# Cross-attention with an adapter branch: the adapter's weighted sums are turned by TensorE and divided in PSUM, instead of by VectorE's 32x32 blocks and a trip through HBM, in a new instruction order

## The chip, the cores and the metric

The kernel runs on one core of one Trainium2 chip. A core has five engines with a queue each: TensorE (PE in the profile, its weight loads PEld), VectorE (DVE), ScalarE (ACT), GpSimd (POOL) and SyncE (SP), which here issues nearly all DMAs. Every queue is worked off in its own order; an instruction that waits holds up everything behind it on its engine. The metric is the device time of one execution in microseconds (us), the median of several runs; the profile is a recording of one further execution.

## The reference, cut to what matters

Two sequences of 2048 rows of 640 numbers (`x`) attend to 124 text tokens each, and a second branch, the adapter, attends from 4 extra tokens to the whole of `x` and is used again. Everything is float32.

```python
query = hidden_states @ Wq
keyt, valt = enc @ Wk, enc @ Wv
hs = _mha(query, keyt, valt)                      # text branch, 8 heads
ca_q1 = jnp.einsum('btc,th->bch', ca, Wq_ca)      # 384 channels of 4 tokens
indices = np.linspace(0, CAD - 1, S).astype(np.int64)
ca_q1 = ca_q1[:, indices, :]                      # 2048 rows, only 384 different
ca_hs1 = _mha(ca_q1, residual, residual)          # first softmax of the adapter, over 2048 keys
ca_q2 = ca_hs1 @ Wq
ca_k2, ca_v2 = ca @ Wk_ca, ca @ Wv_ca
ca_hs2 = _mha(ca_q2, ca_k2, ca_v2)                # second softmax, over 4 tokens
out = (hs + ca_hs2) @ Wout + b_out + residual
```

## The kernel before, in words

**Two branches, 16 units.** Each of the two sequences (b = 0, 1) is cut into four blocks of 512 rows and eight text units of 256 rows (m = 0 to 15, `text`). A unit has scores (`sc`), a softmax (`p`, `r`), a turn of the probabilities by way of HBM (`eb`, `kept`, `pT`), a product with the values (`ph`, copied to `hs`), and the product with `Wout` (`po`), whose pieces VectorE adds to the residual rows (`x_more`, `last_rows`) before they are stored. The queries (`pq`) and the output product use sums of blocks of the operands, so that 7 products do the work of 8.

**The adapter** (`adapter`, L1474) goes through five stages for each b. (1) Scores of the 384 distinct channel rows against the 2048 keys, in 24 pieces of 128x2048 that fill a PSUM region of four banks (`s`); VectorE takes the maximum of each piece (`mx<-s`). (2) The maxima are turned by four 32x32 block transposes on VectorE (`spread`, L1510), sent to HBM and brought back as rows of the operand `cop`. (3) For each half j = 0, 1 of the heads, twelve pieces of scores (`s<-zop,cop`) get their exponential from ScalarE (`ea<-s`), and `contract` (L1584) multiplies them with `y_sb` into one PSUM bank `acc` of 128x384. Its 128 rows are four groups g of 32, in each of which 24 rows are weighted sums (`Y`) and one row is the sum of the exponentials (`ONE`); its columns are the 384 channels. (4) `second` (L1645) needs the channels on the partitions: it adds the sums over groups and halves, which gives the scores `s2f` of the second softmax (over 4 tokens). (5) The probabilities `p2t` are spread over the 2048 rows by a product with a 0/1 matrix (`pt_p<-rows,p2t`), copied, and stored to HBM (`p<-rows`), from where every unit's `pT` fetches its 4 extra rows (`second_rows`, L1867). So no `ph` product of sequence b can run before stage 5 of `adapter(b)`.

**Stages 3 to 4 in the kernel before.** At the end of each `contract(b, j)` VectorE turns `acc` in 32x32 blocks out of PSUM into `accs` (L1607), which frees the bank; then it takes the reciprocals of the exponentials' sums (L1613) and multiplies (L1614), into `prod[:, j]`. Since the blocks are turned each in its place, a channel's four groups still lie on four different partition quarters. So `second` adds the two halves (`both`, L1654), stores them to HBM (`heads_away`, L1662), fetches them back so that all four groups of a channel lie on one partition (`gather`, four DMAs, L1667; the buffer `heads` is the second half of `prod`), and sums them (`less`, L1674: three reductions, a maximum, a subtraction). ScalarE's exponential, a sum, a reciprocal and a product (`share`, L1687) follow, all before PE's `product` (L1706). This happens once for each b.

**The order** of all instructions is written out in the string `ORDER` (L74): 2240 numbers, each the number of a task (a Python generator) whose next step is to be issued; a letter a, v or g chooses the engine where two could do it. Tasks are numbered in the order in which they begin; 36 is `adapter(0)`, 241 is `adapter(1)` in both versions, and 37 + 4m is unit m's `text`, whose `probabilities` (loads of `pT`, then the `ph` products) is 40 + 4m. `Room` objects stand for buffers: there are four single PSUM banks (`banks`) beside the four-bank region until the second adapter is through (`more`, L1699), and two buffers `eas` for `ea` and `accs`.

**Matmul forms.** `Desk.matmul` (L205) issues a product with more than 64 rows and columns as four strips of 32 columns ("128*32" in the profile), except straight after a transpose or another product in the full 128*128 form; then it stays in that form until a product with a smaller shape.

Of the kernel before, what the change touches and what calls it, by code (L numbers as in the profile page):

```python
# [8 lines left out]
F32 = mybir.dt.float32  # L9
# [5 lines left out]
P = 128  # L15
# [51 lines left out]
class Desk:  # L67
# [7 lines left out]
        0 4 4 0 36 2 0 0 0 0 0 0 0 0 0 0 0 0 2 4 2 2 2 4 4 2 2 2 2 2 2 2 2 111v 6 6 6 0 0 112v 6 4 6 3 110 107 109 108  # L75
        4 114a 113a 3a 3 6 3a 3 115v 4 6 7 7 7 7 15 2 15 15 15 12 15 15 15 3v 1 3 116a 117a 8 7 8 11 15 15 10 7 7 7 7
        15 120a 5 6 118a 8 8 9 119v 14 7 7 7 7 121a 123v 8 7 7 36 122a 125a 8 124v 6 8 9 8 8 8 126 5 9 8 8 127 8 5 9 9
        9 36 5 129 14 15 128 130 9 9 9 14 14 14 14 9 6 6 135v 14 134a 133a 132v 14g 14 15 14 12 14g 15 136 36 36 6 11
        6 36 12 12 137 137 137 137 11a 36 15 137 36 36 15 12 12 36 145v 36 9 9 9 140 11 9 9 9 138a 139a 9 144a 12 13
        101 101g 101g 101g 101g 106 141 141 141 141 141 6 141 141 18 142 16 141 141 143 106 18 18 143 131 131 131 131  # L80
        143 143 143 39 146 146 36 36 146 146 146 146 17 17 101g 101v 101 147g 148g 150g 149g 146 143 131 151 17 155a
        17 146g 101g 36 18 18 18 18 18 143 36 101g 16 16 16 16 16 16 151 157a 156 16v 43 36 151 17 159a 156 156 158
        158 158 158 16 16 158 16g 36 146 151 160a 18 156 18 18 18 18 18 152 154 161 36 17 36 154 152 36 154 143 162
        162 162 162 162 18 20 19 21 21 21 21 146 158 156 20 163 36 162 158 164 19 36 36 153 171 36 19 143 19 19 19 19
        177a 167g 168g 170g 158g 178 43 171 153 36 158 36 179 179 181 36 180a 19g 171 165 166 21 21 166 166 21 21 21
        172 166 178 158 179 179 179 179 182a 178 39 183 19 183 21 21 179 179g 169g 36 21 21 21 21 20 23 178 166 183
        183 183 183 19 20 171 20 174 20 176 174 19g 17 166 166 166 22 36 36 179 183 184a 166 173 185 178 185 185 185
        185 24 24 24 179 185 186 183g 36 187 22 24 24 24 24 190 24 24 188 183 183 22 22 22 176 36 47 176 175 22 36 193
        193 193 36 175 194 193 22 193 193 24 173 173 173 173 23 200 23 23 36 204a 193 195 47 36 23 196g 197g 22g 200
        23 198g 193g 199g 24 24 22 24 24 205 205 24 207 20 173 26 173 173 173 205 205 205 22 22g 205 193 36 207 207  # L90
        207 207 203 210a 206a 189 156 207 205 192 36 51 203 36 36 189 27 27 193 27 27 27 27 205g 205 205 189 189 189
        27 192 203 200 213 213 213 213 36 189 215v 213 213 214 213 192 189 201 36 36 200 202 216 201 202 55 213g 213
        217 218 51 219 219 36 27 27 27 26 223g 221g 222g 27 220 220 36 219 219 219 219 219 192 192 189 189 220 220 220
        220 219g 224g 213 225 226 229a 36 227 225 227 226 191 131 156 131 191 131 191 208 191 191 231a 27 27 27 23 156
        36 219 36 27 220 30 232 36 219 220g 55 230a 228 225 36 191 234a 191 26 191 25 29 178 30 30 30 228 233 233 220
        220 156 30 235 225 228 36 36 36 233 191 36 36 209 233 233 233 36 131 36 211 209 59 237 236 238 233 238 233v
        233 25 238 238 25 25 36 238 238 26 59 26 36g 131 209 209 29 36 36 26 242v 243g 25 25 209 209 233 178 240 240
        240 240 36 209 209 209 247 246 238 245v 252v 36 247 36 240 247 246 36 247 253v 246 240 30 30 30 156 30 244v
        238g 212 192 238 238 212 254v 248 248 36 247 247 36 248 248 248 36 246 250 212 239 239 212 248 240 240g 212
        178 257a 36 63 36 212 247 250 247 247 247 36 30 30 239 240 239 260 260 260 260 260 212 30 30 261 25 260 36 30  # L100
        260 30 251 67 36 262 212 247 251 247 251 240 178 192 192 25 178 260g 260 260 10 192 36 36 263 263 264 212 263
        263 263 36 255 258 52 256 32 26 247 31 247 33 33 192 256 32 239 247 29 31 33 36 247 263 31 36 67 36 247 247 31
        36 29 36 29 247 247 29 270 31 271 263 265g 270 263v 263 270 270 36 270 270 36 256 256 256 256 247 272 272 272
        272 272 266v 272 63 277 277 271 33 267v 263 36 247 269 281v 277 277 277 256 36 36 247 247 269 33 31 33 33 11
        33 33 31 256 36 36 256 259 282 282 36 282 277 283v 271 269 36 36 282 249 271 282 282 259 31 247 271 259 259
        270 270v 270 270 259 275 31 31 28 247 247 284v 269 285v 36 249 28 36 36 282 282 31 28 36 286 268v 277 277v 31g
        241 28 71 28 287 28 259 282 36 282 259 36 280 36 288 277 288 289 282 25 25 277 288 288 36 288 25 288 282 280
        282 36 280 282 75 36 36 259 33 282 32 68 33 33 33 33 33 241 259 36 25g 290 288 288v 241 291 291 288 32 282 241
        282 282 32 241 36 32 31 288 273 31 291 291 291 291 36 75 36 291 291v 291 282 29 292 292 292 292 292 292 293
        293 31g 25 287 25 35 25g 28 36 279 241 279 241 293 293 293 293 278 298 241 71 241 282 278 241 282 282 103 35  # L110
        301g 299 299 293 241 10 296 291 299 299 299 68 48 28 294 28 28 28 28v 68 28 274 274 293g 302g 304g 299 300 293
        287 299 305 36 36 311 282 35 35 241 282 309a 35 305 312a 311 282 28 311 299g 241 282 282 310 241 241 35 306
        241 306 271 274 274 274 287 313 313 313 313 239 44 274 274 274 274 56 64 276 313 313 28g 303g 311 241 293 310
        310 68 307 308 319a 311 34 287 102 314 310 310 241 241 305 320a 308 310 241 299 241 310 307 305 310a 308 241
        321 322 241 323 34 241 79 241 241 324 324 241 34 34 34 324 324 324 324 324 315 276 68 276 66 271 66 317 103
        102 105 328g 330g 331g 326g 329g 40 104 48 327g 104 310 276 276 68 68 68 68 68 276 287 40 105 68 241 333a 332a
        79 241 339 241 46 48 48 48 48 34 343 343 34 241 46 38 299 334a 335g 336g 324g 343 343 276 343 343 34 34 276 40
        34 276 295 48 295 40 287 34 337g 338g 345g 34g 344g 341 340 241 340 339 341 339 241 339 324 340 241 241 83 339
        241 346 346 339 241 346 346 346 346 340 346 34 324 339 342 241 342 346g 241 346 48 48 48 241 48 34 348a 351g
        356 241 356 350a 349a 34g 83 241 356 40 40 239 295 295 295 32 295 295 352g 353g 339 359 241 356 359 357 357  # L120
# [119 lines left out]
def kernel(  # L240
# [1404 lines left out]
    def second(b):  # L1645
# [16 lines left out]
        def heads_away():  # L1662
            dma(kept, by_quarter)
# [504 lines left out]
```

## Time and profile before

| | |
|---|---|
| median of 3 runs | 569.17 us (568.46 to 569.74) |
| the profiled execution's own time | 569.77 us |
| its span, first to last instruction | 568.1 us |
| granted TensorE clock | 1.000 |
| PE busy | 553.8 us |
| VectorE busy | 394.0 us |
| ScalarE busy | 263.0 us |
| GpSimd busy | 192.4 us |
| DMA, moved | 102.08 MB, 180 GB/s |

The span is the profiled execution from its first to its last instruction; the 1.7 us between it and the execution's own time lie before and after. In a row of groups, "128x384 f32<-128x384 f32 x4" is the shape written and read and the number of instructions; behind the bar stand their summed and mean time. In a row of the timeline the first two numbers are the start and the length in us, and neighbouring instructions of one kind are put together ("x16"); matmuls overlap in the pipeline, so the start of the next row says more of the rate than the length does. A float32 product counts twice in "x".

### The profile page before, as it was taken

The page shows a single profiled execution, that of the slowest core. Times are in us where ns is not written, and L with a number is a line of the kernel's source. Part 1 is how long each engine was busy: PE and PEld are TensorE (multiplying, and loading weights), DVE is VectorE, ACT ScalarE, POOL GpSimd, SP SyncE. Part 2 cuts the span into 40 slices and gives each one's busy share as a digit, 9 for nine tenths or more (in the row PEclk, how much of TensorE's full clock was granted, in tenths as well). Part 3 has the DMA queues.
Part 4 walks back from the last instruction along what each step waited for, and adds up shares of the span by engine and source line. Part 5 has one row for each costly group of instructions (what it writes and reads, how often), then busy time and mean ns, then how long its engine had stood idle before and what let it go on. Part 6 is the DMA issues. An engine that isn't in the chain of part 4 may idle for free.

```text
span 568.1 us, 18972 instructions
## 1 busy us (share of the span) xinstructions
PE 553.8 (97%) x8148; PEld 297.9 (52%) x8148; DVE 394.0 (69%) x625; ACT 263.0 (46%) x730; POOL 192.4 (34%) x212
## 2 busy tenths in 40 slices
PE   8999899999999999999999899999999999999997
PEld 8563455455664554555454455556545555555453
DVE  2347899999997746688999999637544654545453
ACT  2222544545537889696524433668878212001000
POOL 7002832542513120142649465231230631333220
PEclk9999999999999999999999999999999999999999
DMA  8993847888677878538468796938962669587704
GB/s 262 241 167 99 178 85 146 201 176 177 158 170 176 202 192 185 156 107 251 141 168 200 214 237 166 283 96 234 271 186 78 191 144 254 166 230 197 212 2 186
DMA packets 152996, 102.08 MB, mean 180 GB/s; under 512 B 87660, under 2 KB 131452, under 8 KB 152912
## 3 DMA queue, kind: packets, MB, share of 16 engines
q1 hardware_dynamic: 152144, 100.47, 69.4%
q8 instruction: 64, 1.05, 0.8%
q0 software_dynamic: 768, 0.40, 0.3%
q14 instruction: 20, 0.16, 0.1%
HBM read 61.64 MB, written 39.20 MB: 178 GB/s over the span
## 4 chain that ended last, share of the span: by engine, by line
PE 82%; DVE 5%; DMA 5%; ACT 3%; SPq 2%; issue 1%; POOL 0%; ACTq 0%; DVEq 0%
PE po L211 26%; PE pq L211 23%; PE acc L211 7%; PE ph L211 7%; PE sc L211 6%; PE s L211 6%; DVE mx L226 2%; SPq L236 2%; PE pq_first L211 2%; DMA zb<-z 2%; PE pyz L211 1%; DMA w_kca<-in_L_xattn_Wk_ca_dram 1%; ACT ea L226 1%; PE pk L211 1%; DMA wq_sb<-in_L_xattn_Wq_dram 1%
## 5 line engine op out<-in xcount | busy, mean ns | idle before, releaser
L226 ACT ACTIVATE p<-sc,m 128x124 f32<-128x124 f32 x256 | 90.1, 378 | 48.1 <-DVE m L226 47.9
L226 DVE TENSOR_REDUCE mx<-s 128x4 f32<-128x2048 f32 x48 | 109.3, 2277 | 3.9 <-PE s L211 3.8
L226 ACT ACTIVATE ea<-s 128x2048 f32<-128x2048 f32 x48 | 90.7, 1889 | 26.8 <-PE s L211 26.8
L211 PE MATMUL po<-wout_sums,hs 128*32 128x320 f32 x1024 | 77.6, 433 | 0.4 <-DVE x_more L226 0.4
L211 PE MATMUL po<-wout_sb,hs 128*32 128x320 f32 x992 | 76.6, 433 | 1.1 <-DVE x_more L226 1.1
L226 POOL TENSOR_TENSOR p<-p,r 128x992 f32<-128x992 f32 x21 | 38.8, 1846 | 83.9 <-DVE r L226 83.9
L226 DVE TENSOR_TENSOR last_rows<-last_rows,po 128x320 f32<-128x320 f32 x60 | 28.3, 481 | 49.0 <-PE po L211 49.0
L226 ACT ACTIVATION_READ_ACCUMULATOR p<-sc,m 128x1 f32 x256 | 56.3, 220 | 0.0
L211 PE MATMUL pq<-xt,wq_sb 128*32 128x256 f32 x896 | 54.7, 380 | 0.6 <-ACT p L226 0.6
L226 POOL TENSOR_TENSOR hs<-hs 128x256 f32<-128x256 f32 x40 | 30.6, 771 | 69.9 <-ACT hs L226 37.5
L226 DVE TENSOR_TENSOR x_more<-x_more,po 128x320 f32<-128x320 f32 x68 | 31.8, 481 | 29.4 <-PE po L211 29.1
L211 PEld LDWEIGHTS po<-wout_sums,hs 128*32 128x32 f32 x1024 | 33.0, 110 | 34.1 <-issue 2.6
L211 PE MATMUL acc<-ea,y_sb 128*32 128x384 f32 (+2 forms) x768 | 50.9, 383 | 0.0
L226 DVE TENSOR_REDUCE m<-sc 128x4 f32<-128x496 f32 x64 | 40.0, 660 | 13.4 <-PE sc L211 13.4
L226 ACT COPY hs<-ph 128x512 f32<-128x512 f32 (+1 forms) x27 | 14.2, 551 | 74.8 <-PE ph L211 56.9
L211 PEld LDWEIGHTS po<-wout_sb,hs 128*32 128x32 f32 x992 | 31.7, 110 | 32.6 <-DVE x_more L226 1.8
L211 PE MATMUL ph<-pT,vpad 128*32 128x256 f32 x768 | 46.7, 380 | 0.0
L226 DVE STREAM_TRANSPOSE eb<-p 128x1024 f32<-128x1024 f32 x32 | 39.6, 1237 | 3.1 <-DMA kept<-eb 1.5
L211 PEld LDWEIGHTS pq<-xt,wq_sb 128*32 128x32 f32 x896 | 27.9, 110 | 22.5 <-issue 4.8
L211 PE MATMUL pq<-xt,wq 128*32 128x512 f32 x320 | 39.0, 596 | 0.2 <-ACT p L226 0.2
L211 PE MATMUL sc<-kmain,q 64*128 64x124 f32 x512 | 37.9, 284 | 1.1 <-DVE vpad L226 0.5
L211 PEld LDWEIGHTS sc<-kmain,q 64*128 64x128 f32 x512 | 31.8, 187 | 12.1 <-issue 7.5
(198 smaller groups left out, 789.6 us busy)
## 6 DMA issues: line engine op xcount, KB each, us to landing
kept<-eb SPq DMA_DIRECT2D x32, 512.0 KB, 4.6
pT<-kept SPq DMA_DIRECT2D x48, 256.0 KB, 5.5
landing<-away SPq DMA_DIRECT2D x60, 128.0 KB, 3.5
xi<-in_x_dram SPq DMA_DIRECT2D x28, 256.0 KB, 7.4
x_more<-in_x_dram SPq DMA_DIRECT2D x17, 320.0 KB, 5.7
out_dram<-x_more SPq DMA_DIRECT2D x16, 320.0 KB, 2.2
last_rows<-in_x_dram SPq DMA_DIRECT2D x15, 320.0 KB, 6.8
out_dram<-last_rows SPq DMA_DIRECT2D x14, 320.0 KB, 2.2
```

The source lines that it names most:

```text
L211: self.pin(self.nc.tensor.matmul(out[strip], lhsT[:, strip], rhs, **kw))
L226: return lambda *args, **kw: self.pin(getattr(engine, what)(*args, **kw))
L236: self.pin(self.nc.sync.dma_start(out, in_))
```

## The change: what it does

Stage 3's end and stage 4 are changed for each b and j. ScalarE copies `acc` to `accs` (and so frees the bank); PE turns `accs` by three 128x128 transposes into another PSUM bank `pt_acc`; VectorE's reciprocal and multiplication read that bank. Channels then lie on the partitions with all four groups side by side, so `both`, `heads_away` and `gather` go, and `less` sums over halves and groups at once (8 terms instead of 4). The maxima of stage 2 stay as they were. `ORDER` is another string, of 2238 numbers: each `contract` has one step more (28 instead of 27) and each `second` three fewer.

```diff
     ORDER = """
-        0 4 4 0 36 2 0 0 0 0 0 0 0 0 0 0 0 0 2 4 2 2 2 4 4 2 2 2 2 2 2 2 2 111v 6 6 6 0 0 112v 6 4 6 3 110 107 109 108
...
-        575 548 575 576 563 575 548 579 580 565 576 581 564 583 575 575 584 582 578 578 585 577 577 586
+        2 2 2 2 2 2 36 0 0 0 4 4 0 0 0 0 0 0 0 0 4 0 0 111a 6 6 6 0 4 6 4 2 2 2 2 2 2 2 4 112a 107 108 109 110 4 6
...
+        427 427 411 419v 411 428 241 427 325 429 241 427 428 241 241 427 427 429 428 429 417 241 241 241 428 428 427 427
...
+        448g 445 446v 441v 442v 427 325 427 456 427 444 444 444 444 454 456 99 458 444 456 452 459 456 449v 444a 458
...
+        576 546 576 546 559 560 575 576 577 575 579 580 581 582 547 546 577 575 583 585 584 578 578 586
     """
...
-            late["prod"] = pool.tile([P, 2, 4 * NCC, Y], F32, name="prod")
-            late["heads"] = late["prod"][:, 1].rearrange("p (g a) k -> p g a k", a=NCC)
+            late["prod"] = pool.tile([P, NCC, 2, 4, Y], F32, name="prod")
...
         accs, i = op.value, op.slots[0][0]
-        accs = accs.rearrange("p (n k) -> p n k", k=G)
         yield Do(
-            "DVE", lambda: desk.v_transpose(accs, acc[:, :CAD].rearrange("p (n k) -> p n k", k=G)),
-            frees=[(banks, at)], marks=[("acc done", b, j)]
-        )
-        r = small.tile([P, 4 * NCC], F32, tag="r1", name=f"r1_{b}_{j}")
+            "ACT", lambda: copy(accs, acc[:, :CAD]), frees=[(banks, at)], marks=[("acc done", b, j)]
+        )
+
+        def turn(s):
+            pt = bank(s[0], f"pt_acc_{b}_{j}")
+            for ct in range(NCC):
+                transpose(pt[:, ct * P : (ct + 1) * P], accs[:, ct * P : (ct + 1) * P], ident)
+            return pt
+
+        op = yield Do("PE", turn, needs=[(banks, 1)], frees=[(eas, i)])
+        p4 = op.value[:, :CAD].rearrange("p (a g k) -> p a g k", a=NCC, g=4)
+        r = small.tile([P, NCC, 4], F32, tag="r1", name=f"r1_{b}_{j}")
 
         def divide():
-            desk.v_reciprocal(r, accs[:, :, ONE])
+            desk.v_reciprocal(r, p4[:, :, :, ONE])
             desk.v_tensor_tensor(
-                late["prod"][:, j].rearrange("p (q a) k -> p a q k", q=4),
-                accs[:, :, :Y].rearrange("p (a q) k -> p a q k", q=4),
-                r.rearrange("p (a q x) -> p a q x", q=4, x=1).to_broadcast([P, NCC, 4, Y]), ALU.mult,
-            )
-
-        yield Do("DVE", divide, frees=[(eas, i)], marks=[("prod", b, j)])
+                late["prod"][:, :, j, :, :], p4[:, :, :, :Y],
+                r.unsqueeze(3).to_broadcast([P, NCC, 4, Y]), ALU.mult,
+            )
+
+        yield Do("DVE", divide, frees=[(banks, op.slots[0][0])], marks=[("prod", b, j)])
...
-        def both():
-            desk.v_tensor_tensor(late["prod"][:, 0], late["prod"][:, 0], late["prod"][:, 1], ALU.add)
-
-        op = yield Do("DVE", both, [("prod", b, 0), ("prod", b, 1)])
...
-        def heads_away():
-            dma(kept, by_quarter)
-
-        op = yield Do("SP", heads_away, [op.at])
-
-        def gather():
-            of_quarter = kept.rearrange("(g l) q n -> q l g n", g=4)
-            for q in range(4):
-                dma(late["heads"][G * q : G * (q + 1)].rearrange("l g a k -> l g (a k)"), of_quarter[q])
-
-        op = yield Do("SP", gather, [op.at])
-
         def less():
             for ct in range(NCC):
                 desk.v_tensor_reduce(
-                    s2f[:, ct, :, 1:], late["heads"][:, :, ct, :].rearrange("p g (h t) -> p h t g", t=T1),
+                    s2f[:, ct, :, 1:],
+                    late["prod"][:, ct, :, :, :].rearrange("p j g (h t) -> p h t (j g)", t=T1),
                     AX.X, ALU.add,
                 )
...
-        yield Do("DVE", less, [op.at])
+        yield Do("DVE", less, [("prod", b, 0), ("prod", b, 1)])
```

In the new string `contract(b, j)` is task 251, 282, 390 and 427 (before: 247, 282, 381 and 414); 444 is `second(1)`, 312 is `second(0)`; 456, 454 and 458 are chains of `po` products of a unit.

More of the change, by code (lines that the diff above doesn't have):

```diff
@@ L80 @@
[L80 to L99, printed above, removed]
@@ new lines @@
+        84 479 433g 452 96 96 96 500 480 496g 495g 497v 96 486 507v 500 433 96 505a 487 485 76 94 92 96 506 94 92 92
+        76 76 504 499 76 76 74 517v 518g 508a 485 488 485 501 500 513 510v 500 487 511g 513 501 500 513 486 513 513
+        513 486 512g 500 509g 514 501 485 74 76 76 521g 514 522v 520v 513 514 76 76 500 525g 523v 488 498v 526v 530
+        524a 531 503 500 529 502 92 519 433 90 533 72 501 92 92 90 72 534 72 72 503 460 529 460 72 527g 529 529 514
+        530 513 537 515 92 92 92 529 538a 515 539v 542v 516 528v 529 529 532 72 72 540v 70 92 100 100 100 535v 541v
```

126 lines of the change are left out of this document (69 added, 57 removed).

## The prediction

> **What bounds the kernel now.** I read the page's totals first, then the busy time by stage, then PE's waits.
>
> ```profile
> span 568.1 us, 18972 instructions
> PE 553.8 (97%) x8148; PEld 297.9 (52%) x8148; DVE 394.0 (69%) x625; ACT 263.0 (46%) x730; POOL 192.4 (34%) x212
> PEclk9999999999999999999999999999999999999999
> PE 82%; DVE 5%; DMA 5%; ACT 3%; SPq 2%; issue 1%; POOL 0%; ACTq 0%; DVEq 0%
> ```
>
> PE is busy for 553.8 of 568.1 us at the full granted clock, and the chain of waits runs through it for 82% of the span. So an edit counts by two things: PE work that it adds or takes away, and the 14.3 us in which PE is idle. Where those are (columns: stretch, its length, busy time of PE, PEld, DVE, ACT, POOL):
>
> ```profile
> 0.00:50.00 50.00, 47.17 (x408) 31.31 (x412) 20.32 (x78) 11.28 (x21) 14.31 (x54) 1.00 0.83 203
> 50.00:100.00 50.00, 48.18 (x686) 23.75 (x680) 45.38 (x53) 22.30 (x81) 20.36 (x20) 1.00 0.65 133
> 100.00:300.00 200.00, 197.74 (x3054) 106.78 (x3056) 163.18 (x222) 126.36 (x366) 66.31 (x56) 1.00 0.72 176
> 300.00:350.00 50.00, 46.67 (x648) 24.56 (x648) 49.78 (x53) 23.41 (x97) 31.88 (x27) 1.00 0.88 218
> 350.00:550.00 200.00, 200.00 (x3164) 104.98 (x3160) 108.67 (x208) 79.67 (x168) 59.54 (x56) 1.00 0.67 183
> 550.00:569.00 19.00, 14.03 (x212) 6.50 (x200) 6.69 (x15) 0.00 (x0) 0.00 (x0) 1.00 0.37 139
> 300.00:325.00 25.00, 21.67 (x289) 11.61 (x289) 24.86 (x26) 12.73 (x56) 16.49 (x13) 1.00 0.79 210
> ```
>
> From 350 to 550 us PE has no gap at all. The largest hole in the middle is 25 - 21.67 = 3.3 us between 300 and 325, where VectorE is full (24.86 of 25): the second adapter's maxima. PE's waits:
>
> ```profile
> PE s L211 <- DVE mx L226: 2.2, 5, 0.8
> PE po L211 <- DVE x_more L226: 1.4, 2, 1.1
> ...
> PE pt_x L219 <- DMA xz<-in_x_dram: 0.5, 1, 0.5
> ...
> PE s L211 <- ACT ea L226: 0.4, 2, 0.2
> ...
> PE p_kca L211 <- DMA w_kca<-in_L_xattn_Wk_ca_dram: 0.2, 1, 0.2
> ```
>
> The only DMAs that PE is seen to wait for are the first loads. The trip through HBM that the change removes is not among them.
>
> **What the removed trip costs now.** The chain of sequence 1, from the last `acc` product to the product `pt_p` (PE and VectorE rows of the timeline, in order of time):
>
> ```profile
> 440.26 1.05 PE L211 MATMUL acc<-ea,y_sb 128*32 128x128 f32 x16
> 441.44 0.58 DVE L226 STREAM_TRANSPOSE accs<-acc 128x384 f32<-128x384 f32 x1 [3.33 <-PE acc L211]
> 442.06 0.23 DVE L226 RECIPROCAL r<-accs 128x12 f32<-128x12 f32 x1
> 442.32 0.46 DVE L226 TENSOR_TENSOR prod<-accs,r 128x288 f32<-128x288 f32 x1
> 442.81 0.89 DVE L226 TENSOR_TENSOR prod<-prod 128x288 f32<-128x288 f32 x1
> 451.48 0.77 DVE L226 TENSOR_REDUCE s2f<-prod 128x24 f32<-128x96 f32 x3 [1.25 <-DMA prod<-heads]
> ...
> 454.48 1.07 PE L211 MATMUL pt_p<-rows,p2t 128*32 128x512 f32 x12
> ```
> ```profile
> 441.30:454.50 13.20, 13.20 (x212) 6.68 (x205) 9.64 (x24) 2.04 (x8) 7.82 (x11) 1.00 0.67 192
> ```
>
> The trip takes 451.48 - 443.70 = 7.8 us of a chain of 13.2 us, and PE is busy for all 13.2 with other units' `po` and `ph`. Removing it is therefore worth 0 on PE, as long as the earlier start of `ph` fills no hole. (If that cover were gone, the trip would cost its 7.8 us.)
>
> **Part 1: twelve transposes on PE.** Rows of transposes of the same shape and type at the start of the kernel:
>
> ```profile
> 18.88 0.66 PE L219 MATMUL pt_wq<-ident,wq_sb 128*128 128x128 f32 x4
> 19.37 0.27 PE L219 MATMUL pt_wq<-ident,wq 128*128 128x128 f32 x1
> ...
> 23.46 0.60 PE L219 MATMUL pt_wq<-ident,wq_sb 128*128 128x128 f32 x4
> 23.90 0.27 PE L219 MATMUL pt_wq<-ident,wq 128*128 128x128 f32 x1
> ```
> ```profile
> L219 PE MATMUL pt_wq<-ident,wq_sb 128*128 128x128 f32 x20 | 3.0, 277 | 0.0
> ```
>
> Four in a row take 23.90 - 23.46 = 0.44 us from start to start, 0.11 each; straight behind a product in strips (`p_kca`) they take 19.37 - 18.88 = 0.49, so the change of form costs 0.05. A turn of three is 3 x 0.11 + 0.05 = 0.38 us, four turns are 1.5 us. PE has no room to hide this: the turns stand among work that already fills it. The lower end is 1.3 (no cost of the form), the upper 4 x (3 x 0.277 + 0.05) = 3.5 (nothing overlaps); I take 1.5, since the rows show transposes in a row. In "TensorE: Matmul & The Clock Gate", section "Part 4: PE-mode transpose", the Trainium skill gives about 275 ns for a 128x128 bf16 transpose inside a kernel, which matches the 277 ns mean length here; by it as a price the twelve would be 3.3 us, but the starts 0.11 us apart speak for 1.5. After a turn, wide products stay in the 128*128 form for a while; no row prices these shapes in both forms, and I take 0, between -0.3 and +0.3.
>
> **Part 2: ScalarE's copy and PE's wait for it.** VectorE loses four block transposes (0.58), two sums (0.89 at most) and gains longer reductions: 8 terms for 4, so 0.77 becomes at most 1.5 per b. Net about -2.3 - 1.4 + 1.4 = -2.3 us, off the path except between 300 and 325. ScalarE gains four copies of 128x384. The nearest rows:
>
> ```profile
> L226 ACT COPY hs<-ph 128x512 f32<-128x512 f32 x21 | 12.3, 596 | 70.8 <-PE ph L211 52.8 <-issue 18.0
> L226 ACT COPY hs<-ph 128x256 f32<-128x256 f32 x6 | 2.4, 392 | 4.0 <-PE ph L211 4.0
> L226 ACT ACTIVATE ea<-s 128x2048 f32<-128x2048 f32 x48 | 90.7, 1889 | 26.8 <-PE s L211 26.8
> ```
>
> Halfway, 0.49 us each. The new wait is PE's: a turn cannot start before the copy, and everything behind it on PE stands. For the last turn the new order puts one two-product step of `po` between the last `acc` product and the turn; and between the turn and `pt_p` (entries 1868 and 1879) stand the second step of chain 456 and the first steps of 454 and 458. Their lengths:
>
> ```profile
> 451.25 1.26 PE L211 MATMUL po<-wout_sums,hs 128*32 128x320 f32 x16
> 452.32 1.80 PE L211 MATMUL po<-wout_sb,hs 128*32 128x320 f32 x24
> 453.94 0.72 PE L211 MATMUL po<-wout_sb,wout_sums 128*32 128x320 f32 x8
> ```
>
> A step of 16 instructions holds PE for 452.32 - 451.25 = 1.07 us, one of 24 for 1.62. Cover for the copy: 1.07 us against 0.13 (end of `acc` at 441.31 to VectorE's start at 441.44, as a hand-over) + 0.49 + 0.15 = 0.8: no wait if ScalarE is free. Cover for the chain behind the turn: 1.07 + 2 x 1.62 = 4.3 us, against reciprocal and product 0.23 + 0.46, `less` to `pt_p` as now 454.48 - 451.48 = 3.0, the longer reductions 0.4 to 0.7, and hand-overs 0.2: 4.3 to 4.6. So the wait there is 0 to 0.3. If ScalarE has just begun an `ea` exponential when a copy becomes ready, that copy is up to 1.9 us late, and PE loses up to 1.6 us; queued behind are `po` and score products, and VectorE's sums wait for these. I take 0.3 for all waits together; the ends are 0 and 4 x 1.6 = 6.4. The turned bank is held until the division; after the first turn that stands 53 entries later in the order, which leaves three banks for the queries. Its bounds are 0 and PE's longest wait for a `po` sum now, 1.1; I take 0.
>
> **Part 3: SP and the order.** Ten small DMAs and their issues go. PE waits for no `pT` now, so this is worth 0 in the steady part (at the most the same hole between 300 and 325). The new order replaces all positions. What it can gain is bounded by the holes: 3.3 us at 300 to 325, 2.8 + 1.8 us in the first 100, 2.3 from 100 to 300. It can also open such holes of the same size. Three readings of the string say that the layout is the same: the first `ph` of sequence 0 (task 68) stands behind 12 of the second adapter's 24 maxima in both; the `pt_p` of sequence 1 is entry 1889 before and 1879 now, with 350 and 358 entries behind it; and `adapter(1)` ends with entry 1818 before, 1826 now. The time won by the shorter chain has been spent on a later adapter, not on earlier products. I take 0, with -3.3 and +3.3 as ends.
>
> **The sum.** Against the profiled execution's own 569.77 us: + 1.5 (turns) + 0.3 (waits) + 0 (order) = 571.6. That execution lies 0.6 above the median of the runs, 569.17, so the forecast for a median is **571.0 us**, 0.3% slower.
>
> **The rivals.**
>
> *The order closes the hole of the maxima (faster).* Place: 300 to 325 us. With the trip gone, `second(0)` can be through 7 us earlier and `ph` and `po` of sequence 0 can stand between the pieces `s`, where PE now waits 2.2 us for `mx`; VectorE is also relieved a little. For it: VectorE's 24.86 of 25 us there. Against it: the twelve maxima ahead of the first `ph` in both orders. It decides once more than 1.8 us of the 3.3 go. All gone: 571.0 - 3.3 = 567.7. Chance 0.15.
>
> *The gain and the cost cancel.* Half of that hole goes, 1.7 us: 571.0 - 1.7 = 569.3. Chance 0.17.
>
> *PE stands at the turns.* Copies come behind `ea` exponentials of 1.89 us in stage 3, where ScalarE is busiest, and the chain before `pt_p` comes out longer. Four waits of about 1 us: 571.0 + 4 = 575.0. For it: one step of 1.07 us as the only cover at the last turn. Against it: PE waits 0.4 us for `ea` now, since the order leaves room. Chance 0.13.
>
> *Transposes at full length.* Twelve that hold PE for 0.277 each instead of 0.11, so + 2.0: 573.0. Against it: starts 0.11 us apart. Chance 0.04. (This is what the Trainium skill's figure in "Part 4: PE-mode transpose", above, would make of it.)
>
> **How the numbers follow.** The forecast has a chance of 0.51, with a range of its own from 570.0 to 572.8 (turns 1.3 to 2.5, waits 0 to 1, order -1 to +1). A run of this kernel can tell about 0.2%, 1.1 us, from no change: below 568.0 is faster, above 570.3 slower. Faster: 0.15 and a little of the second rival, 0.17. Slower: 0.45 of the forecast's 0.51, and the last two rivals, 0.62. Same: the rest, 0.21. The range of 8 in 10 goes from 567.6, which takes in the closed hole, to 575.0.
>
> **What would show it.** Right: PE's busy time up by 1.3 to 2.5 us with twelve transposes of about 0.28 us, PE still without a gap between 350 and 550, its idle time within 2 us of 14.3. The first rival: PE idle below 11.5, the stretch 300 to 325 full. The third: a new row among PE's waits, `pt_acc` waiting for ScalarE or `pt_p` for VectorE, of over 2 us. The forecast falls if idle time moves by more than 3 us either way.

## The result and the profile after

The changed kernel takes 565.65 us (median of 19 runs, 564.78 to 569.48) against 568.70 us for the kernel before on the same chip (19 runs, 567.69 to 570.23): a ratio of 0.9949, interval 0.9939 to 0.9959. It is 0.5% faster, where 571.0 us, 0.3% slower, was forecast; the time lies below the range too.

The page of the changed kernel (span, busy time by engine, the chain that ended last):

```profile
span 564.1 us, 18793 instructions
PE 554.7 (98%) x8064; PEld 314.1 (56%) x8064; DVE 387.5 (69%) x622; ACT 265.3 (47%) x732; POOL 198.5 (35%) x211
PE 90%; DVE 5%; DMA 1%; ACT 1%; issue 1%; SPq 1%; DVEq 0%; ACTq 0%
```

PE does 0.9 us more work (554.7 for 553.8), as a change that adds transposes must, and is idle for 9.4 us instead of 14.3. The 4.0 us that the span lost are these two: + 0.9 - 4.9. So the question is which gaps closed. The windows of the changed kernel, then those two of the kernel before that the prediction doesn't show (columns as there):

```profile
0.00:200.00 200.00, 196.58 (x2670) 112.30 (x2674) 151.68 (x249) 93.41 (x304) 77.19 (x107) 1.00 0.75 173
200.00:300.00 100.00, 99.01 (x1448) 51.86 (x1442) 74.45 (x101) 68.57 (x164) 32.24 (x26) 1.00 0.67 170
300.00:350.00 50.00, 48.69 (x706) 25.58 (x708) 48.83 (x59) 24.65 (x100) 29.76 (x26) 1.00 0.83 218
350.00:550.00 200.00, 200.00 (x3102) 118.39 (x3098) 105.88 (x201) 78.64 (x166) 59.35 (x54) 1.00 0.67 185
300.00:325.00 25.00, 23.68 (x342) 12.83 (x344) 24.83 (x29) 14.21 (x58) 15.93 (x13) 1.00 0.87 243
```
```profile
0.00:200.00 200.00, 194.61 (x2632) 110.30 (x2634) 154.90 (x251) 91.66 (x304) 70.25 (x98) 1.00 0.76 175
200.00:300.00 100.00, 98.47 (x1514) 51.55 (x1514) 73.98 (x101) 68.28 (x162) 30.73 (x33) 1.00 0.64 170
```

Idle time of PE (length less busy time) goes from 5.39 to 3.42 in the first 200 us, from 1.53 to 0.99 between 200 and 300, and from 3.33 to 1.31 between 300 and 350; from 350 to 550 it is 0 in both. The last 0.4 us lie at the end. Two places matter: the **head**, ahead of the first turn (222.6 us), with 2.0 us, and the **hole of the maxima** with 2.0 us. In the hole VectorE is as full as before (24.83 of 25 us, before 24.86): PE has more to do beside it.

The parts of the change itself came out nearly as priced. The timeline of PE at the last turn of the changed kernel, and its groups of turns and copies:

```profile
438.80 1.05 PE L211 MATMUL acc<-ea,y_sb 128*32 128x128 f32 x16
439.67 1.26 PE L211 MATMUL po<-wout_sb,hs 128*32 128x320 f32 x16
440.86 0.55 PE L219 MATMUL pt_acc<-ident,accs 128*128 128x128 f32 x3
441.24 1.78 PE L211 MATMUL po<-wout_sb,hs 128*128 128x320 f32 x6
442.86 1.24 PE L211 MATMUL po<-wout_sums,hs 128*128 128x320 f32 x4
444.03 1.16 PE L211 MATMUL sc<-kmain,q 64*128 64x124 f32 x16
...
447.16 1.07 PE L211 MATMUL pt_p<-rows,p2t 128*32 128x512 f32 x12
```
```profile
L219 PE MATMUL pt_acc<-ident,accs 128*128 128x128 f32 x12 | 2.2, 291 | 0.0
L226 ACT COPY accs<-acc 128x384 f32<-128x384 f32 x4 | 1.9, 482 | 1.5 <-PE acc L211 1.5
```

A turn holds PE for 441.24 - 440.86 = 0.38 us, ScalarE's copy takes 0.48, and PE waits for neither. From the end of the last `acc` (439.85) to `pt_p` there are 7.3 us; before there were 13.2.

### The profile page after: what moved, and what is told of

The parts are those of the page before. It is cut to its first block, busy times and chain, and to the rows that moved or that the text cites. A ratio compares the mean times of both kernels' runs of the same rounds, so it can differ in the third digit from the quotient of the medians.

```text
span 564.1 us, 18793 instructions
## 1 busy us (share of the span) xinstructions
PE 554.7 (98%) x8064; PEld 314.1 (56%) x8064; DVE 387.5 (69%) x622; ACT 265.3 (47%) x732; POOL 198.5 (35%) x211
## 4 chain that ended last, share of the span: by engine, by line
PE 90%; DVE 5%; DMA 1%; ACT 1%; issue 1%; SPq 1%; DVEq 0%; ACTq 0%
PE po L211 26%; PE pq L211 25%; PE acc L211 8%; PE sc L211 7%; PE ph L211 7%; PE s L211 7%; PE pq_first L211 3%; DVE mx L226 3%; PE pyz L211 3%; PE pk L211 1%; PE unread L215 1%; DMA first_rests<-away 1%; DVE m L226 1%; SPq L236 1%; PE pt_wq L219 1%
## 5 line engine op out<-in xcount | busy, mean ns | idle before, releaser
L226 POOL TENSOR_TENSOR p<-p,r 128x992 f32<-128x992 f32 x28 | 51.9, 1857 | 132.3 <-DVE r L226 126.6
L211 PE MATMUL po<-wout_sums,hs 128*32 128x320 f32 (+1 forms) x1012 | 77.8, 433 | 0.5 <-DVE x_more L226 0.5
L226 DVE TENSOR_TENSOR x_more<-x_more,po 128x320 f32<-128x320 f32 x72 | 33.6, 480 | 44.4 <-PE po L211 44.4
L211 PEld LDWEIGHTS po<-wout_sums,hs 128*32 128x32 f32 (+1 forms) x1012 | 37.6, 110 | 29.5 <-issue 1.4
L211 PEld LDWEIGHTS po<-wout_sb,hs 128*32 128x32 f32 x956 | 36.3, 111 | 27.5 <-issue 0.9
L226 POOL TENSOR_TENSOR hs<-hs 128x256 f32<-128x256 f32 x35 | 26.9, 776 | 60.4 <-DVE hs L226 52.0
L226 DVE TENSOR_TENSOR last_rows<-last_rows,po 128x320 f32<-128x320 f32 x56 | 26.1, 478 | 22.2 <-PE po L211 22.0
L226 ACT COPY hs<-ph 128x512 f32<-128x512 f32 (+1 forms) x23 | 12.1, 541 | 59.2 <-PE ph L211 59.0
L211 PEld LDWEIGHTS sc<-kmain,q 64*128 64x128 f32 x512 | 31.9, 187 | 11.7 <-issue 7.5
```

The costliest lines, as they stand in the source:

```text
L211: self.pin(self.nc.tensor.matmul(out[strip], lhsT[:, strip], rhs, **kw))
L226: return lambda *args, **kw: self.pin(getattr(engine, what)(*args, **kw))
```

## The experiments

The order is a string, so the two versions differ in two things that can be taken apart: the code, and the order in which each step is issued. In the experiments the steps of one order were matched by their meaning with those of the other ("new order" is that of the changed kernel, "old order" that of the kernel before), and put together from parts of both: the first N entries of the one, then what is left in the sequence of the other. All kernels compute the reference in full. Where an order was cut, steps meet that were not planned for each other, and waits stand at the seam; they are named. Of the `ORDER` diffs only the first changed line is shown.

**1. The changed code in the old order.** The first kernel puts each turn one PE step behind the copy; the second, with mended places, leaves more.

```diff
-        2 2 2 2 2 2 36 0 0 0 4 4 0 0 0 0 0 0 0 0 4 0 0 111a 6 6 6 0 4 6 4 2 2 2 2 2 2 2 4 112a 107 108 109 110 4 6
+        0 4 4 0 36 2 0 0 0 0 0 0 0 0 0 0 0 0 2 4 2 2 2 4 4 2 2 2 2 2 2 2 2 111v 6 6 6 0 0 112v 6 4 6 3 110 107 109 108
...
```


> The changed code in the order of the kernel before: every step keeps its place, a turn stands one PE step behind its copy, the division one VectorE step behind the turn, and the reductions stay where the trip through HBM had put them. If the gain came from the order (theory A), the holes of before stay and the turns come on top: PE busy 555, idle 13 to 15, 569 to 571 us. If it came from the trip's removal itself, whatever the order (theory B), the time is that of the changed kernel, 564 to 567 us.

573.21 us, ratio 1.0076 (1.0060 to 1.0092), above the 569 to 571 that were expected if the gain came from the order. PE waited 1.3 us for one copy, and 0.8 and 0.7 us for `hs` and `last_rows`, which had come to stand late. With the places mended:

```diff
-        293 287 299 305 36 36 311 282 35 35 241 282 309a 35 305 312a 311 282 28 311 299g 241 282 241 282 241 282 35
+        293 287 299 305 36 36 311 282 35 35 241 282 309a 35 305 312a 311 282 28 311 299g 241 282 241 241 35 282 306
...
```


> As e1, with the places of three turns and divisions mended: the turn of sequence 0's second half stands two PE steps behind its copy, and the last division two VectorE steps behind its turn. If e1's 4.2 us over the kernel before were the turns (1.9 us of PE) and waits of my own placing (about 2 us), this takes 570.5 to 572 us, which is what the prediction's sum gave for the change in an unchanged layout. If the code itself costs more in the old order, 573 again.

571.75 us, ratio 1.0049 (1.0035 to 1.0063), of which about 1.4 us are waits at the places that were chosen here (0.3 for a copy, 0.8 and 0.3 for `hs`). Its windows:

```profile
0.00:200.00 200.00, 194.13 (x2638) 109.92 (x2640) 155.19 (x251) 91.82 (x304) 70.42 (x98) 1.00 0.76 175
300.00:350.00 50.00, 46.72 (x656) 24.64 (x644) 49.94 (x51) 23.44 (x97) 32.47 (x28) 1.00 0.89 222
```

Head and hole are as empty as before (5.87 and 3.28 us idle; the head of the first kernel, in the same order, has 4.26, so one trace can differ from the next by 1.6 us there). So the code by itself, in the layout that the prediction had assumed, closes no gap. It takes 3.1 us more than the kernel before on the same chip (571.75 and 568.69), or 1.7 without those waits, where the prediction's sum gave 1.8. The difference to the changed kernel, 5.7 us by the ratios, is the order, with 1.4 of it owed to the places chosen here.

**2. The old code in the new order,** with no entry out of its place; then the same with the second product six PE steps later.

```diff
-        0 4 4 0 36 2 0 0 0 0 0 0 0 0 0 0 0 0 2 4 2 2 2 4 4 2 2 2 2 2 2 2 2 111v 6 6 6 0 0 112v 6 4 6 3 110 107 109 108
+        2 2 2 2 2 2 36 0 0 0 4 4 0 0 0 0 0 0 0 0 4 0 0 111a 6 6 6 0 4 6 4 2 2 2 2 2 2 2 4 112a 107 108 109 110 4 6
...
```


> The code before (block transposes, trip through HBM) in the changed kernel's order, the two sums and the trip issued straight behind the second division, everything else in its place. Both theories expect PE to stand before the two products pt_p, since the chain of about 13 us now has 7 us of cover: about 4 to 6 us each, 4.4 to 4.8 us less by the turns being gone is 1.5, so 572 to 577 us. If the order needs no shorter chain (theory A in its strong form), under 567.

587.27 us, ratio 1.0322 (1.0288 to 1.0357), 10 us above what was expected. The trip is no longer hidden, in either sequence; beside its two waits PE stands 1.6 us for `accs` and 1.2 for `rows`. PE's and VectorE's waits in its timeline (the release stands in brackets):

```profile
293.21 0.80 PE L211 MATMUL s<-zop,cop 32*128 32x512 f32 x4 [4.82 <-DVE mx L226]
...
462.64 1.95 PE L211 MATMUL pt_p<-rows,p2t 128*32 128x512 f32 x12 [7.24 <-DVE p2t L226]
```
```profile
289.62 0.76 DVE L226 TENSOR_REDUCE s2f<-prod 128x24 f32<-128x96 f32 x3 [5.11 <-DMA prod<-heads]
...
459.85 0.76 DVE L226 TENSOR_REDUCE s2f<-prod 128x24 f32<-128x96 f32 x3 [8.53 <-DMA prod<-heads]
```

In sequence 0 VectorE stands 5.1 us for `gather`, and the maxima behind it in its queue are what PE then waits for; in sequence 1 PE waits for the probabilities themselves. So in this order, with the trip straight behind the division, a long chain costs two waits that the short one doesn't have.

```diff
-        29 282 313 282 28 35 314 300 313 28g 315 282 48 282 282 308 316a 241 241 296 308 312 312 312 312 241 312 317a
+        29 282 313 282 28 35 314 300 313 28g 315 282 48 282 282 308 316a 241 241 296 308 312 312 312 241 317a 241 313
...
```


> As e2, but the second softmax and pt_p stand six PE steps (about 8 us) later in the changed kernel's order, and what needs them moves behind. Theory A (any order as good as the new one would have done, also with the trip): 564.5 to 567 us. Theory B (the short chain is what lets the first ph products come in time for the hole of the maxima): 568 us or more, the hole between 300 and 325 back to about 3 us or wider.

602.13 us, ratio 1.0571 (1.0551 to 1.0592): now the first `ph` of each sequence waits for its probabilities (8.9 and 4.1 us), since `ph` had hardly been moved with them. It says that a product can't be moved alone, and nothing on how well the old code could be packed.

**3. The turns twice.**

```diff
-            for ct in range(NCC):
+            for ct in [*range(NCC)] * 2:
```


> The changed kernel with each turn done twice into the same bank: twelve transposes more on PE. At 0.11 us each, with the form already changed, +1.3 us: 566.9 to 567.2 us. If transposes hold PE for their full 0.28 us, +3.4: 569. If PE has slack at the turns, no change: 565.6.

567.81 us, ratio 0.9986 (0.9974 to 0.9998): by the ratios 2.1 us over the changed kernel for twelve more transposes, where 1.3 were expected. The intervals of the two ratios leave 1.2 to 3.0 us. Busy time of PE rises by 0.6 and idle time between 300 and 350 by 0.9. Transposes in a row are cheap but not hidden: 0.05 us each by the busy time, 0.18 by the whole time (0.10 to 0.25), around the 0.11 of the prediction.

**4. The head alone.** The old code with the first 880 entries (210 us) in the new order, then the changed code with those entries in the old order.

```diff
-        0 4 4 0 36 2 0 0 0 0 0 0 0 0 0 0 0 0 2 4 2 2 2 4 4 2 2 2 2 2 2 2 2 111v 6 6 6 0 0 112v 6 4 6 3 110 107 109 108
+        2 2 2 2 2 2 36 0 0 0 4 4 0 0 0 0 0 0 0 0 4 0 0 111a 6 6 6 0 4 6 4 2 2 2 2 2 2 2 4 112a 107 108 109 110 4 6
...
```


> The code before, trip and all; the first 880 entries (about 210 us, ahead of the first turn and of everything that the diff touches) in the new order, the rest in the old. Theory A (the new order is better packed also where the change plays no part): 1.5 to 2.5 us faster than before, 566.3 to 567.3. Theory B (only what the short chain allows is gained): 568.7 to 569.2.

567.74 us, ratio 0.9989 (0.9974 to 1.0005): 0.6 us faster by the ratio, and not clear of no change, where 1.5 to 2.5 were expected. There is a wait of 2.1 us at the seam (`sc` for `yz`), and 48 `ph` products at half the granted clock take 1.3 us longer than before (last section). Its head:

```profile
0.00:200.00 200.00, 196.89 (x2684) 112.41 (x2688) 152.31 (x249) 94.14 (x304) 77.20 (x107) 1.00 0.77 172
```

3.11 us idle for 5.39, with the code of before.

```diff
-        2 2 2 2 2 2 36 0 0 0 4 4 0 0 0 0 0 0 0 0 4 0 0 111a 6 6 6 0 4 6 4 2 2 2 2 2 2 2 4 112a 107 108 109 110 4 6
+        0 4 4 0 36 2 0 0 0 0 0 0 0 0 0 0 0 0 2 4 2 2 2 4 4 2 2 2 2 2 2 2 2 111v 6 6 6 0 0 112v 6 4 6 3 110 107 109 108
...
```


> The changed code; the first 880 entries in the old order, the rest in the new. Theory A: 1.5 to 2.5 us over the changed kernel, 567.2 to 568.2. Theory B: as the changed kernel, 565.3 to 566.0.

567.35 us, ratio 0.9981 (0.9971 to 0.9992): by the ratios 1.8 us over the changed kernel, with the head at 5.53 us idle and the hole closed:

```profile
0.00:200.00 200.00, 194.47 (x2628) 110.18 (x2630) 154.72 (x251) 91.02 (x304) 69.92 (x98) 1.00 0.76 175
300.00:350.00 50.00, 48.52 (x696) 25.32 (x684) 48.83 (x53) 23.55 (x94) 31.36 (x26) 1.00 0.87 227
```

So the head packed anew is part of the gain, and it hangs on no line of the changed code. All traces of this case bear it out: PE's idle time in the first 200 us is 4.1 to 5.9 us in the six kernels with the old order there (5.0 in the mean) and 3.0 to 3.9 in the eleven with the new one (3.4), with either code. By these means the head is worth 1.6 us, a little less than the 2.0 of the two traces above.

**5. Cuts at entry 1250, around the second product of sequence 0** (290 to 300 us). Old order up to there with the changed code; then new order up to there with the changed code, with sequence 1 by the old trip, and with the old code.

```diff
-        36 29 36 29 247 247 29 270 31 271 263 56 241 40 28 44 256 60 33 272 33 271 33 33 256 270 256 263g 265g 266g
+        36 29 36 29 247 247 29 270 31 271 263 265g 270 263v 263 270 270 36 270 270 36 256 256 256 256 247 272 272 272
...
```


> The changed code; the first 1250 entries (about 300 us: past the first sequence's pt_p, ahead of the first ph) in the old order, the rest in the new. Against s2 it tells what the stretch from 210 to 300 us is worth, and against e4 what everything behind 300 us is worth. Theory A, with the holes spread evenly: 568.5 to 569.5. If most of the gain comes behind 300 us (the hole of the maxima, theory B): 566 to 567.5.

573.59 us, ratio 1.0076 (1.0057 to 1.0095), above both ranges that were expected, with 2.9 us of waiting for `mx` behind the first `ph`: the time says little.

```diff
-        46 277 34 320 34 277 304 331 310g 327g 329g 328g 68 68 334a 68 241 335a 330g 311g 338g 339g 332g 340g 337g 34
+        46 277 52 239 331 331 331 331 331 331 320 266 102 327g 329g 330g 310g 328g 311g 277 68 68 68 277 287 40 105 68
...
```


> The changed code; the first 1250 entries (the head and sequence 0 to the second softmax) stand in the changed kernel's order, the rest in the order of before, with the turns of sequence 1 at places of my own. If the gain lies in the order up to and around sequence 0's adapter (the theory): 566 to 567.5 us, the changed kernel's 565.65 and up to 1.5 us of waits at my own places; PE idle at most 1.5 us over the changed kernel's 9.4. If the tail of the order carries a good part of the gain (the rival): 568.5 us or more.

571.70 us, ratio 1.0054 (1.0035 to 1.0072). What was expected of the theory fell: the order behind entry 1250 matters as well. Head 3.19 us idle, hole 3.88; 1.3 us of the hole is a wait for `p` at the seam, and three waits of the kernel before are there again (below).

```diff
+        if b == 1:
+            accs = accs.rearrange("p (n k) -> p n k", k=G)
+            yield Do(
+                "DVE", lambda: desk.v_transpose(accs, acc[:, :CAD].rearrange("p (n k) -> p n k", k=G)),
...
+            op = yield Do("SP", heads_away, [op.at])
...
+            op = yield Do("SP", gather, [op.at])
...
```


> Sequence 0 by TensorE's turns as in the changed kernel, sequence 1 by VectorE's blocks and the trip through HBM as in the kernel before; the first 1250 entries in the changed kernel's order, the rest in that of before. If the trip of sequence 1 lies wholly beside work of PE (the theory): six transposes and two changes of form less on PE, its busy time 0.7 to 0.9 us below the changed kernel's 554.7, and 564.5 to 565.5 us. If the short chain is needed at sequence 1 too (the rival): a wait for p2t or pT of over 1 us there, and 567 us or more.

570.41 us, ratio 1.0014 (0.9999 to 1.0030), with 2.1 us of waiting for `last_rows` at 512 us; 0.85 us less PE work than the kernel ahead of it, as six transposes less make it, and 1.3 us faster than it on the same chip. No wait for `p2t` or `pT` in sequence 1. The expected 564.5 to 565.5 was missed for the same reason as above, the cut.

```diff
-        0 4 4 0 36 2 0 0 0 0 0 0 0 0 0 0 0 0 2 4 2 2 2 4 4 2 2 2 2 2 2 2 2 111v 6 6 6 0 0 112v 6 4 6 3 110 107 109 108
+        2 2 2 2 2 2 36 0 0 0 4 4 0 0 0 0 0 0 0 0 4 0 0 111a 6 6 6 0 4 6 4 2 2 2 2 2 2 2 4 112a 107 108 109 110 4 6
...
```


> The code of before, both sequences through the trip; the first 1250 entries in the changed kernel's order, the rest in that of before. Beside m1 this differs in sequence 0's turns alone. If the changed order around sequence 0's adapter needs the short chain (the theory): the wait of some 7 us at the first pt_p that the full splice had, less what PE's copies saved give back, so 570 to 573 us. If that wait came of other parts of the full splice (the rival): within 1 us of m1, 564 to 566.5.

576.59 us, ratio 1.0122 (1.0100 to 1.0144), above the 570 to 573 that were expected, and 6.2 us over the one before it, from which it differs in sequence 0's turns alone:

```profile
294.48 0.80 PE L211 MATMUL s<-zop,cop 32*128 32x512 f32 x4 [5.21 <-DVE mx L226]
```

At sequence 0, with the adapter as late as the new order has it, the short chain is worth its 5 us.

**6. Cuts where both orders have nearly the same steps behind them.** Changed code, new order to entry 1775; sequence 1 by the trip, new order to 1715; then the old code with its trips in the old places and only entries 1225 to 1775 in the new order, and the same with the new head too.

```diff
-        428 241 325 427 427 417 428 99 241 241 96 427 427 241 427 56 56 429 417 417v 423g 422g 433 417 433 431 431 241
+        56 56 417 426g 422g 409 423v 241 427 427 241 76 427 325 417 429 241 241 427 99 241 428 92 427 427 432 241 325
...
```


> The changed code in the changed order up to entry 1775, the rest in the order of before. If the gain lies ahead of it (head and hole of the maxima): 565.5 to 567 us, and the stretch from 300 to 325 us as full as the changed kernel's 23.68. If the tail carries part of it: 568 us or more.

568.52 us, ratio 0.9991 (0.9978 to 1.0005). The time is over the 568 that stood for the tail, but the hole is full (1.06 us idle between 300 and 350), and there are 1.85 us of waits for `ea` (424.9 us) and `hs` (442.2 us) at the seam, where the changed kernel has none.

```diff
-        46 277 52 239 331 331 331 331 331 331 320 266 102 327g 329g 330g 310g 328g 311g 277 68 68 68 277 287 40 105 68
+        46 277 34 320 34 277 304 331 310g 327g 329g 328g 68 68 334a 68 241 335a 330g 311g 338g 339g 332g 340g 337g 34
...
```


> Sequence 0 by TensorE's turns, sequence 1 by blocks and the trip; the changed order up to entry 1715, the order of before behind it, so that the trip has its old places. If sequence 1's turns bring nothing but their own price: PE busy 0.7 to 0.9 us under the changed kernel's, 564.5 to 565.5 us. If the short chain is needed there: a wait of over 1 us for what the trip brings, 567 us or more.

568.05 us, ratio 0.9986 (0.9966 to 1.0005), with 2.5 us of waits for `ea` and `last_rows`. Not slower than its sister with the turn, and not the better kernel that was hoped for: PE's busy time is 555.8 us, 1.1 above the changed kernel's instead of 0.7 to 0.9 below it, with the granted clock at 0.99 between 350 and 550 us.

```diff
-        321 322 241 323 34 241 79 241 241 324 324 241 34 34 34 324 324 324 324 324 315 276 68 276 66 271 66 317 103
+        321 322 241 323 34 241 79 241 241 40 60 66 66 32 276 276 34 34 34 310 317 68 68 68 105 103 104 104 48 324 241
...
```


> The code of before with both trips at their old places; only entries 1225 to 1775 (behind the first second product, around the hole of the maxima) stand in the changed order. If closing the hole needs the short chain at sequence 0 (the theory): 300 to 325 us as empty as before (at most 22.2 of 25) and 568 to 570 us. If the order of these entries closes it alone (the rival): over 23 of 25, and 566 to 567 us.

571.98 us, ratio 1.0056 (1.0036 to 1.0077), above both ranges that were expected, with 1.6 us of waiting for `accs` and 1.0 for `ea` behind the hole. PE is idle for 2.19 us between 300 and 350 instead of 3.33, but the hole isn't half closed for that: the granted clock falls to 0.50 there, and 48 `ph` products that take 2.80 us in the kernel before take 4.16 (rows below).

```diff
-        0 4 4 0 36 2 0 0 0 0 0 0 0 0 0 0 0 0 2 4 2 2 2 4 4 2 2 2 2 2 2 2 2 111v 6 6 6 0 0 112v 6 4 6 3 110 107 109 108
+        2 2 2 2 2 2 36 0 0 0 4 4 0 0 0 0 0 0 0 0 4 0 0 111a 6 6 6 0 4 6 4 2 2 2 2 2 2 2 4 112a 107 108 109 110 4 6
...
```


> As the run before, with the changed order in the first 880 entries too. If order alone is what gains (the rival): 564.5 to 566 us, the changed kernel's time or less without a line of its code. If the hole needs the short chain (the theory): 567 to 569 us, what the new head alone gave.

572.77 us, ratio 1.0068 (1.0049 to 1.0087), above both ranges, with 4.5 us idle between 300 and 350. Set beside 6's third, which has the same code and the same steps in the hole, it shows what the half clock hid there. `ph`, and the second piece `s` behind it, in 6's third and then in this one:

```profile
303.54 4.16 PE L211 MATMUL ph<-pT,vpad 128*32 128x256 f32 x48
...
310.90 0.50 PE L211 MATMUL s<-zop,cop 32*128 32x512 f32 x4
```
```profile
304.87 2.89 PE L211 MATMUL ph<-pT,vpad 128*32 128x256 f32 x48
...
312.27 0.50 PE L211 MATMUL s<-zop,cop 32*128 32x512 f32 x4 [1.26 <-DVE mx L226]
```

At the full clock `ph` is through 1.3 us sooner, and PE then waits 1.26 us for `mx`: from `ph` to this `s` 7.4 us pass in both. So with the old code, the new order behind `ph` alone closes nothing.

**What closes the hole, read wait by wait.** The times of cut orders carry their seams, but the waits between 300 and 350 us stand in each trace under their own names. In the kernel before, PE ahead of the first `ph` of sequence 0 (the `acc` and `pt_p` products first):

```profile
277.59 1.07 PE L211 MATMUL acc<-ea,y_sb 128*32 128x128 f32 x16
...
294.55 1.08 PE L211 MATMUL pt_p<-rows,p2t 128*32 128x512 f32 x12
...
298.15 0.51 PE L211 MATMUL s<-zop,cop 32*128 32x512 f32 x4
...
301.05 0.50 PE L211 MATMUL s<-zop,cop 32*128 32x512 f32 x4 [0.32 <-DVE mx L226]
...
303.95 0.51 PE L211 MATMUL s<-zop,cop 32*128 32x512 f32 x4 [0.76 <-DVE mx L226]
304.39 2.80 PE L211 MATMUL ph<-pT,vpad 128*32 128x256 f32 x48
```

and in the changed kernel:

```profile
281.12 1.07 PE L211 MATMUL acc<-ea,y_sb 128*32 128x128 f32 x16
...
290.53 1.07 PE L211 MATMUL pt_p<-rows,p2t 128*32 128x512 f32 x12
...
297.29 0.51 PE L211 MATMUL s<-zop,cop 32*128 32x512 f32 x4
...
301.09 0.51 PE L211 MATMUL s<-zop,cop 32*128 32x512 f32 x4
301.90 2.84 PE L211 MATMUL ph<-pT,vpad 128*32 128x256 f32 x48 [0.30 <-DMA pT<-kept]
```

Before, the last pieces `s` ahead of `ph` come 2.90 us apart, which is all that VectorE does between two of them; the steps that PE has between them are too few, and it waits 0.32 and 0.76 us. After, `s` comes 3.80 us apart and finds the region free, and `ph` is there 2.5 us earlier.

- These **two waits** stand (0.32 or 0.33, and 0.77) again in the kernels with the old code and the old places there (experiment 4's first, 6's third) and in the changed code in the old order too (1's second, 5's first). They are gone where both the code and the order around the second product are new (4's second, 5's second and third, 6's first two). With the old code in the new order (2's first, and 5's last) waits of 1.2 and 4.8 to 5.2 us stand there instead. So in the orders that were tried these 1.1 us need code and order together.
- The **waits behind the first `ph`** (before: 0.39 and 0.32 for `mx`, 0.37 and 1.05 for `x_more`, 2.1 us) stand with the old order behind entry 1225 or 1250, with either code (0.31, 0.32, 0.38 and 1.05 in experiment 1's second; 0.45, 0.32, 0.37 and 1.04 in 4's first). With the new order there they are 0.47 for `x_more` and 0.26 for `p` in the changed kernel, and the same within 0.1 us in 4's second and 6's first two. But the new order there isn't enough: where the two old waits stand ahead of `ph`, those behind it are 2.90, 0.15 and 0.28 with the changed code (5's first) and 1.26, 0.54, 1.10 and 0.16 with the old code (6's last), 3.1 to 3.3 us and not 2.1. In 6's third they are 0.25, 0.74 and 0.16, after the half clock had taken up 1.3 us. With the old code they were small at the full clock in one kernel, 2's first (0.55, 0.17 and 0.16), behind a wait of 4.8 us. So the 2 us of the hole came without another wait only where the code is new for sequence 0 and the order is new both ahead of the first `ph` and behind it.

**What stays open.** The head, 1.6 to 2.0 of the 4.9 us, hangs on the order and not on the code. Whether the old code could have had the hole too, with one order planned for it as a whole, wasn't shown: each combination that was tried brought waits of 1 us and more of its own. Nor is sequence 1's turn shown to gain anything: before, its trip was covered. Of the two pairs with and without it, the first is 1.3 us faster with the trip (571.70 and 570.41), the second 0.5 us (568.52 and 568.05, intervals overlapping, and cut at different entries). No version tried beats the changed kernel.

## Why the prediction was wrong

**The step that failed is Part 3: "I take 0, with -3.3 and +3.3 as ends", for the new order.** PE's idle time fell by 4.9 us, more than the lower end, which named only the hole of the maxima. It failed twice.

- *"Three readings of the string say that the layout is the same."* They were counts of steps, and the same count hides a shift in time. The first `ph` stands behind 12 of 24 maxima in both; yet from the end of `acc` to it there were 304.39 - 278.66 = 25.7 us and are 301.90 - 282.19 = 19.7. "The time won by the shorter chain has been spent on a later adapter" holds for 3.5 of these 6.0 us (the `acc` ends at 282.19 for 278.66); the other 2.5 brought `ph` forward into the hole. The readings for sequence 1 were right and beside the point, since PE has no gap there.
- *The head.* The bounds listed 2.8 + 1.8 us of idle time in the first 100 and 2.3 up to 300, but the ends of -3.3 and +3.3 took in none of it, and no reason was given. A new string replaces the head as well; it packed it 2.0 us tighter in the first 200 us of these two traces, 1.6 in the mean of all (experiment 4).

The first rival had the right place and mechanism for the hole, and its test came out: the stretch from 300 to 325 went from 21.67 to 23.68 and PE's idle time below 11.5. It asked for 3.3 us of the hole and got 2.0. The time came out below its 567.7 all the same, since the head, which it didn't name, gained as much, and PE's work rose by 0.9 and not by 1.5.

**Right: Part 1,** by the row. The twelve transposes take 0.38 us a turn, as priced; but PE's total rose by 0.9 us, not by 1.5, and so less than the 1.3 to 2.5 that were to show it. In the old order (experiment 1's second) it rose by 1.3. The Trainium skill's figure in "TensorE: Matmul & The Clock Gate", section "Part 4: PE-mode transpose", fits the row's mean length again (291 ns in float32 for its 275 in bf16), but as a price it is too high: twelve more in experiment 3 cost 2.1 us (1.2 to 3.0), not 3.3. Wide products behind a turn in the 128*128 form cost nothing extra that the rows show.

**Right: Part 2,** nearly. The copy of 0.48 us was priced at 0.49, and the new kernel has no wait for it. The wait of up to 0.3 us ahead of `pt_p` didn't come: between the last turn and `pt_p` lay 447.16 - 441.24 = 5.9 us of work and not 4.3, since a step of scores (24 `sc`, 1.5 us) had been overlooked in the string. The reductions took a little more than "at most 1.5":

```profile
442.20 1.68 DVE L226 TENSOR_REDUCE s2f<-prod 128x24 f32<-128x192 f32 x3
```

**Right: "removing it is worth 0 on PE, as long as the earlier start of `ph` fills no hole".** With the old order the trip was indeed covered (experiment 1: the changed code gains nothing there). But the condition decided: the earlier start did fill a hole. And the sentence "if that cover were gone, the trip would cost its 7.8 us" is experiment 2's 7.2 us.

## What to carry to other kernels

Here, with PE 97% busy, shortening a hidden chain was worth nothing by itself, and what a new order made of it was worth more than the change cost. So price the order from the idle time that it could close, everywhere that it is new, instead of calling it 0. Compare two orders by the time between events (end of `acc` to first `ph`), not by counting the steps between them. Cutting two orders together tests little by its time, as a seam costs 1 to 3 us; the named waits in the trace tell which part acts, if the granted clock is looked at beside them: a product at half the clock counts as busy time and can hide a wait.

## What the runs showed of the hardware

A short wait of PE can cost more than its length: in two traces the granted clock fell to half behind one. The timeline of PE in the old code with the new order around the hole (experiment 6's third), windows of the same kernel (the granted clock is the third number from the end), and a window of the kernel before:

```profile
302.85 0.76 PE L211 MATMUL s<-zop,cop 32*128 32x512 f32 x4 [0.77 <-DVE mx L226]
303.54 4.16 PE L211 MATMUL ph<-pT,vpad 128*32 128x256 f32 x48
```
```profile
302.00:304.00 2.00, 1.23 (x13) 0.48 (x16) 2.00 (x5) 0.00 (x0) 2.00 (x2) 0.74 0.98 191
304.00:306.00 2.00, 2.00 (x24) 0.95 (x20) 2.00 (x2) 0.41 (x1) 0.88 (x1) 0.50 0.93 259
```
```profile
302.00:304.00 2.00, 1.24 (x26) 1.10 (x22) 2.00 (x2) 0.03 (x1) 2.00 (x2) 1.00 0.92 257
```

Behind waits of 0.32 and 0.77 us the clock was at 0.50 for some 3 us in the one, and 48 `ph` products took 4.16 us instead of 2.80. In experiment 4's first they took 4.12, and from the `s` behind the second wait to the next `s` that waits 11.7 us passed (302.98 to 314.68) instead of 10.45 (303.95 to 314.40) in the kernel before. The same two waits left `ph` at 2.80 to 2.89 us in five kernels: the kernel before, both of experiment 1, 5's first and 6's last. What made the difference isn't shown. After the 7.24 us wait of experiment 2 `pt_p` took 1.95 us for 1.07. The Trainium skill, "TensorE: Matmul & The Clock Gate", section "Part 1: The HAM clock gate (the "warmup" mystery)", gives half the clock after an idle window of about 3.4 us that runs free of the kernel; the half clock agrees with these rows, but in two traces here it came behind 1.1 us of waits within 4 us.
